# Later sums, later weight splits and earlier weight loads around the boundary of two stages of a mixture-of-experts kernel

## The chip, the core and the metric

The kernel runs on one core of one Trainium2 chip. The metric is the device time of one execution in microseconds (us); lower is better. Engines are named as in the profile: PE (matmuls, with PEld for the loads of the stationary operand), DVE (vector), ACT (scalar), POOL (GpSimd) and SP (the sync engine, which here only starts DMAs and loads registers).

## The reference

4096 tokens of width 512 pass through two blocks, each with a residual sum:

```
x = x + ffn0(moe0(x))     # moe0: (shared expert + two of eight routed experts) / 3
x = x + rnn1(moe1(x))     # moe1: one of sixteen experts by token id; rnn1: a gated recurrence
```

What matters here is the first line:

```
shared = (silu(x @ sw1.T) * (x @ sw3.T)) @ sw2.T            # 1024 hidden units
moe0   = (shared + g0 * O[e0] + g1 * O[e1]) / 3             # routed rows O, gates g0, g1
sel    = argmax(policy(moe0[:, last token of the sequence])) # one of 8 experts per sequence
h      = gelu(moe0 @ W1[sel] + b1[sel]);  r = h @ W2[sel] + b2[sel]
x      = x + moe0 + 0.3 * (r @ Wo + bo)
```

After it, `moe1` needs `sigmoid(xr @ w_recept.T)` of a mix of neighbouring tokens. A sequence is 128 tokens long; there are 32 sequences, so 32 blocks of 128 tokens.

## The kernel before

Matmuls are done in three passes on numbers split into a high and a low part (`mm3`, L66). A split (`split`, L61) is two instructions: ACT casts the source to the high part (L63), DVE subtracts it from the source (L64). Every weight and every activation goes through such a split before PE can read it.

The work stands in stages, and the change touches two of them.

**The second half of the shared expert with the sums** (L886 to L946, `shared` at L204). It runs over the four groups 4 to 7 of 512 tokens, and in each over 8 chunks of 128 hidden units, numbered 32 to 63 in all. `up` (L209) of a chunk makes two PSUM tiles `p` of 12 matmuls each; ACT and DVE turn them into the activation (`sg` at L220 to L222) and split it (`as`, L224). `down` of the chunk before (L227) adds 12 matmuls into four accumulators `acc`. The weights of these chunks are loaded once, in group 4: `fetch_sw` (L165) two chunks ahead into six raw buffers, `split_sw` (L171) one chunk ahead, into tiles `kept_u` and `kept_d` that stay for groups 5 to 7.

Beside it, `combine` (L735) does the sum for a block of 128 tokens: DVE scales the first routed row and adds the shared part (L738), adds the second routed row (L739), PE transposes the result (`pth`, L742), ACT divides by three (L744) and stores it, DVE adds the residual (L749), and SP stores that. Its inputs come from `get_o` (L718), two sums ahead, into three buffers each: two row gathers started by POOL (L722), and loads of the shared part and of x started by SP (L729, L732). The list `when` (L901 to L910) says how many sums stand behind each chunk; `hook2` (L925) does the first sum of a chunk behind it, `between` (L920) a second one within the next chunk.

In the last group `hook2` also finds the experts of the first 24 sequences (`policy`), starts the first three gathers of expert weights (`fetch_w`, L847, of 1 MB each, into three raw buffers `rawB`), and splits them (`split_w`, L866) behind chunks 4 to 6: `W1a`, `W1b` and `W2a` of the first sequence. A split frees its raw buffer, so that the gather three places later can start; the fourth and fifth gathers are for the second sequence and move nothing when its expert is the same, the sixth is `W2b`.

**The experts** (L949 to L1224). A loop over sequences b (L1156) runs `up`, `bend` (transpose, gelu, split), `down` of neighbouring sequences in turn; `used` (L1151) splits the weights three uses ahead, under a condition that skips the split when the expert does not change. In the passes b = 0 and b = 1, `weight_b` (L967) loads `Wo` and `w_recept` through the buffers `dx` and `xk` and splits them on the spot (L1170 to L1173). `Wo` is first used by `close` after b = 3, `w_recept` later still.

The order on each engine is not that of the source: a scheduler orders the instructions at build time by priorities and its own estimates of durations, and an engine then runs its list strictly in that order. `tc.issue_after(ins)` queues what is recorded within it behind `ins` on the engine of `ins`; it adds no wait.

Of the kernel before, what the change touches and what calls it, by code (L numbers as in the profile page):

```python
# [1 line left out]

# [6 lines left out]
F32 = mybir.dt.float32  # L9
# [6 lines left out]
ALU = mybir.AluOpType  # L16
# [4 lines left out]
P = 128  # L21
D = 512
KD = D // P
# [10 lines left out]
KF = F1 // P  # L34
# [14 lines left out]
def tile_kernel(ctx: ExitStack, tc: tile.TileContext, a: dict, out: bass.AP):  # L49


    nc = tc.nc
# [7 lines left out]

    def split(hi, lo, src):  # L61

        nc.scalar.copy(hi, src)  # L63
        return nc.vector.tensor_tensor(lo, src, hi.bitcast(F32), ALU.subtract).ins  # L64

    def mm3(ps, left, right, kd, start=True, stop=True):  # L66

# [78 lines left out]
    with ExitStack() as sa:  # L146
# [13 lines left out]
        NSW = KF * NG  # L160
        KEPT = KF * (NG // 2)
        sw_raw, sw_hl, x_raw, xhl = {}, {}, {}, {}
        kept_u, kept_d = {}, {}

        def fetch_sw(n, which=range(3)):  # L165
# [38 lines left out]
        def shared(groups, pools, hook, done, mid=None, before_last=None, more=False):  # L204


            tp, ps_acc, ps_mm = pools
            acts, accs = {}, {}

            def up(n):  # L210
                g, c = divmod(n, KF)
                up, dn = sw_hl.pop(n)
                ps = []
                for w in range(2):
                    ps.append(ps_mm.tile([P, GT], F32, tag="mm", name=f"p{w}_{n}"))
                    mm3(ps[w], lambda h, k: up[:, h, w, k, :], lambda h, k: xhl[g][k][:, h, :], KD)
                    if mid is not None:
                        mid(n, w)
                sg = tp.tile([P, GT], F32, tag="sg", bufs=1, name=f"sg_{n}")
                nc.scalar.activation(sg, ps[0], AF.Sigmoid)  # L220
                nc.vector.tensor_tensor(sg, sg, ps[0], ALU.mult)
                nc.vector.tensor_tensor(sg, sg, ps[1], ALU.mult)  # L222
                act = tp.tile([P, 2, GT], FR, tag="act", bufs=2, name=f"as_{n}")
                split(act[:, 0], act[:, 1], sg)  # L224
                acts[n] = (act, dn)

            def down(n):  # L227
                g, c = divmod(n, KF)
                if c == 0:
                    accs[g] = [ps_acc.tile([P, D], F32, tag="acc", name=f"acc_{g}_{j}") for j in range(GB)]  # L230
                act, dn = acts.pop(n)
                for j in range(GB):
                    mm3(
                        accs[g][j], lambda h, k: act[:, h, bass.ts(j, P)], lambda h, k: dn[:, h, :], 1,
                        c == 0, c == KF - 1,
                    )
                if c == KF - 1:
                    done(g, accs.pop(g))

            first, last = groups[0] * KF, (groups[-1] + 1) * KF - 1  # L240
            for n in range(first, last + 1):
                g, c = divmod(n, KF)
                up(n)
                if c == KF - 1 and (n < last or more):
                    split_x(g + 1)
                if n > first:
                    down(n - 1)
                if n < last:
                    split_sw(n + 1)
                if n + 1 < last:  # L250
                    fetch_sw(n + 2)
                hook(g, c)
                if c == (KF - 2 if n < KEPT + KF else 3) and (g < groups[-1] or more):
                    fetch_x(g + 1)
            if before_last is not None:
                before_last()
            down(last)
# [587 lines left out]
        AHEAD = 3  # L845
# [20 lines left out]
        def split_w(i):  # L866

            if i < len(todo):
                raw = raws.pop(i)
                kind, b = order[todo[i]]  # L870
                if b == 0:
                    ws[kind] = wh.tile([P, 2, KD, D], FR, tag="w", name=f"wB_{kind}")
                if b not in (0, PARTS[0]) and b not in changed:
                    changed[b] = nc.values_load(
                        new_i[0:1, b : b + 1], engines=[nc.scalar.engine, nc.vector.engine],
                        min_val=0, max_val=1,
                    )
                flat = ws[kind].rearrange("p h k n -> p h (k n)")
                with tc.If(changed[b] != 0) if b in changed else nullcontext():
                    for q in range(2):  # L880
                        s = bass.ts(q, KD * D // 2)
                        split(flat[:, 0, s], flat[:, 1, s], raw[:, s])
                fetch_w(i + AHEAD)


        with ExitStack() as s2:  # L886
            dn_p = s2.enter_context(tc.tile_pool(name="dn_p", bufs=2, side="right", **kw))
            split_sw(KEPT)
            pad2 = dn_p.tile([P, 320 // 4], F32, bufs=1, name="pad2")
            nc.gpsimd.memset(pad2, 0.0)  # L890
            tp = s2.enter_context(tc.tile_pool(name="tp2", bufs=2, **kw))
            cp = s2.enter_context(tc.tile_pool(name="cp", bufs=2, **kw))
            sm = s2.enter_context(tc.tile_pool(name="sm", bufs=1, **kw))
            ps_acc = s2.enter_context(tc.tile_pool(name="ps_acc2", bufs=4, space=PSUM, **kw))
            ps_mm = s2.enter_context(tc.tile_pool(name="ps_mm2", bufs=3, space=PSUM, **kw))
            ps_t = s2.enter_context(tc.tile_pool(name="ps_t2", bufs=1, space=PSUM, **kw))
            pools = (tp, ps_acc, ps_mm)


            h, last = NG // 2, NG - 1  # L900
            rest, flat, when = list(range(h * GB)), [], {}  # L901
            for g in range(h, NG):
                own = list(range((g - 1) * GB, g * GB)) if g > h else []
                for c in range(KF):
                    n = (2 if 0 < c < 3 else 0) if g == last else 1
                    n += (g == last - 1 and c == KF - 1) - (g == h and c == 0)
                    when[g, c] = []
                    for _ in range(n):
                        when[g, c].append((own if own and c > 0 else rest).pop(0))
                    flat += when[g, c]  # L910

            def sums(g, c):
                if when.get((g, c)):
                    b = when[g, c].pop(0)
                    combine(b, ps_t)
                    n = flat.index(b) + 2
                    if n < len(flat):
                        get_o(flat[n], cp, 3)

            def between(n, w):  # L920

                if w == 0:
                    sums(*divmod(n - 1, KF))

            def hook2(g, c):  # L925
                sums(g, c)
                if g == last:
                    if c == 0:
                        policy(0, PARTS[0], sm, ps_t)
                        for n in range(AHEAD):  # L930
                            fetch_w(n)
                    if 4 <= c < 4 + AHEAD:
                        split_w(c - 4)

            def keep(g, accs):
                for j in range(GB):
                    b = g * GB + j
                    shs[b] = cp.tile([P, D], F32, tag="sh", bufs=6, name=f"shc_{b}")
                    nc.scalar.copy(shs[b], accs[j])
                    if g == last:  # L940
                        i = h * GB + j
                        nc.scalar.dma_start(out=sh_d[i * P : (i + 1) * P, :], in_=shs[b])

            get_o(flat[0], cp, 3)
            get_o(flat[1], cp, 3)
            shared(range(h, NG), pools, hook2, keep, between)  # L946


    with ExitStack() as sb:  # L949
# [14 lines left out]
        PB = 2  # L964
        HF = F1 // 2

        def weight_b(name):  # L967
            pair = wb.tile([P, 2, KD, D], FR, tag=name, name=f"{name}_hl")
            flat = pair.rearrange("p h k n -> p h (k n)")
            given = a[name].rearrange("p k n -> p (k n)")  # L970
            for q, tag in enumerate(("dx", "xk")):
                s = bass.ts(q, KD * D // 2)
                raw = bp.tile([P, KD * D // 2], F32, tag=tag, name=f"raw_{name}{q}")
                nc.sync.dma_start(out=raw, in_=given[:, s])
                split(flat[:, 0, s], flat[:, 1, s], raw)
            return pair

# [178 lines left out]
        for b in range(-1, NB + 1):  # L1156
# [10 lines left out]
                used()  # L1167
            if b == -1:
                fetch_xh(0)
            if b == 0:  # L1170
                wo0 = weight_b("Wo")
            if b == 1:
                wrec = weight_b("w_recept")  # L1173

            late, step = divmod(b - 3, 3)
            if 0 <= late < GB and step == 0:
# [4 lines left out]
                policy(PARTS[0], NB, cb, ps_t)  # L1181
            if b + 1 < NB:
                bend(b + 1, "a")

            pair = b - 3 if b % 2 and 0 <= b - 3 < NB - 2 else None
            if pair is not None:
# [43 lines left out]
    with ExitStack() as sd:  # L1230
# [86 lines left out]
        AHEAD, RAW = 8, 6  # L1317
# [384 lines left out]
```

## Time and profile before

| what | us |
|---|---|
| median of three runs | 2541.81 (2541.47 to 2545.81) |
| the profiled execution, own time | 2535.17 |
| its span, first to last instruction | 2533.5 |
| PE busy in the span | 2460.9 |
| DVE busy | 1332.4 |
| ACT busy | 1064.2 |
| POOL busy | 428.5 |

The sums' stage stretches from 554.9 us of the span (first matmul of chunk 32) to 847.1 us, the experts' from there to about 1475 us. How to read the lines below: a timeline row is the start, the duration, engine, line, operation, the tile written `<-` the tiles read, and in brackets how long the engine had been idle and who ended that. A row of the windows view is the stretch, its length, the busy time of PE, PEld, DVE, ACT and POOL with the number of instructions, the clock granted to PE as a share of full speed, the share of DMA engine time, and GB/s. A row of the waits view is who waited for whom, the total, the number of times, and the longest.

### The profile page before, as it was taken

Reading aid. Unit: us, or ns where it says so; the run is one execution under the profiler, and the core shown is the slowest. Engines: PE = TensorE matmul, PEld = TensorE weight load, DVE = VectorE, ACT = ScalarE, POOL = GpSimd, SP = SyncE. Lnnn points to the kernel's source line nnn. Section 1 sums busy time; section 2 is a strip of 40 time slices with the busy share of each in tenths; the row PEclk is TensorE's granted clock in tenths of the full one; section 3 lists DMA queues with packets and bytes.
Section 4 is the critical chain, followed back from the end, with each engine's and each line's share of the span. In section 5 each row is a group of like instructions: output and inputs, shape, how many; then the busy total and the mean of one; then the engine's idle time right before and its main releaser. Section 6 shows DMA issues by size and latency. Waiting matters only on the chain. (4 is left out here: it accounts for less than half of the span.)

```text
span 2533.5 us, 37051 instructions
## 1 busy us (share of the span) xinstructions
PE 2460.9 (97%) x13044; PEld 2077.8 (82%) x13044; DVE 1332.4 (53%) x2341; ACT 1064.2 (42%) x1935; POOL 428.5 (17%) x460
## 2 busy tenths in 40 slices
PE   8999999999999899999999999999999999999996
PEld 6788899887887787888887889999978888888885
DVE  7796645556557344445444477667643333333336
ACT  5445533443224445445455466666532222222214
POOL 1000022222223223322322110000010000000003
PEclk9999999999999999999999999999999999999998
DMA  5545544557555333332243387776441111111027
GB/s 181 162 132 172 172 156 152 169 184 254 180 177 169 113 97 126 113 116 99 85 143 116 105 283 238 230 229 224 152 162 42 38 38 38 38 42 46 25 78 267
DMA packets 193116, 351.11 MB, mean 139 GB/s; under 512 B 37472, under 2 KB 72336, under 8 KB 189856
## 3 DMA queue, kind: packets, MB, share of 16 engines
q1 hardware_dynamic: 141504, 244.42, 29.0%
q0 software_dynamic: 36160, 74.90, 10.0%
q10 hardware_dynamic: 15264, 29.37, 3.3%
q8 instruction: 108, 1.77, 0.3%
q14 instruction: 80, 0.66, 0.1%
HBM read 373.94 MB, written 88.13 MB: 182 GB/s over the span
## 5 line engine op out<-in xcount | busy, mean ns | idle before, releaser
L64 DVE TENSOR_TENSOR wD<-rawD,wD 128x1024 fp32r<-128x1024 f32 x128 | 156.5, 1229 | 77.7 <-ACT wD L63 77.7
L71 PE MATMUL p<-xhl,swu 128*128 128x512 f32 x768 | 189.0, 397 | 5.3 <-ACT xhl L63 5.3
L71 PE MATMUL p<-xhl,kept_u 128*128 128x512 f32 x768 | 185.6, 397 | 0.7 <-DVE kept_u L64 0.7
L71 PEld LDWEIGHTS phD<-xe,wD 128*128 128x128 f32 x1536 | 184.7, 189 | 1.8 <-ACT xe L63 0.6
L71 PE MATMUL phD<-xe,wD 128*128 128x256 f32 x1536 | 185.7, 281 | 0.5 <-ACT xe L63 0.5
L71 PE MATMUL poD<-wD,hD 128*128 128x512 f32 x768 | 181.3, 392 | 0.0
L71 PEld LDWEIGHTS p<-xhl,swu 128*128 128x128 f32 x768 | 144.7, 191 | 36.5 <-ACT xhl L63 5.6
L71 PEld LDWEIGHTS p<-xhl,kept_u 128*128 128x128 f32 x768 | 143.3, 190 | 30.5 <-DVE kept_u L64 1.1
L71 PEld LDWEIGHTS poD<-wD,hD 128*128 128x128 f32 x768 | 141.9, 188 | 28.4
L63 ACT CAST wD<-rawD 128x1024 fp32r<-128x1024 f32 x128 | 133.2, 1047 | 53.6 <-PE poD L71 31.0
L266 POOL DMA_INDIRECT xg<-in_x_rows_dram,blk_t x71 | 67.5, 951 | 461.3 <-PE ptx L276 257.4
L1384 POOL DMA_INDIRECT y<-res_d,gat_i x32 | 32.2, 1005 | 575.0 <-DVE r L1403 496.2
L71 PE MATMUL pur<-r,xb 128*128 x852 | 117.8, 287 | 0.9 <-ACT xb L63 0.4
L71 PE MATMUL por<-r,hbr 128*128 x426 | 116.3, 407 | 1.2 <-ACT hbr L63 1.1
L64 DVE TENSOR_TENSOR xb<-ptx,xb 128x512 fp32r<-128x512 f32 x71 | 49.1, 691 | 115.3 <-ACT xb L63 113.7
L71 PEld LDWEIGHTS pur<-r,xb 128*128 128x128 f32 x852 | 104.9, 189 | 2.0 <-ACT xb L63 0.9
L71 PE MATMUL acc<-kept_d,as 128*128 128x512 f32 x384 | 96.1, 400 | 5.1 <-DVE as L64 3.1
L71 PE MATMUL poF<-z,wo_hl 128*128 128x512 f32 x384 | 96.5, 399 | 0.0
L71 PE MATMUL ps_f<-wf_hl,z 128*128 128x512 f32 x384 | 96.4, 399 | 0.0
L71 PE MATMUL ps_c<-wc_hl,z 128*128 128x512 f32 x384 | 94.9, 395 | 0.7 <-issue 0.7
L71 PE MATMUL acc<-swd,as 128*128 128x512 f32 x384 | 95.0, 392 | 0.0
L71 PE MATMUL pb<-rT,Wo_hl 128*128 128x256 f32 x768 | 94.6, 281 | 0.0
(1014 smaller groups left out, 5040.0 us busy)
## 6 DMA issues: line engine op xcount, KB each, us to landing
rawD<-in_w_key_dram SPq DMA_DIRECT2D x64, 512.0 KB
rawD<-in_w_value_dram SPq DMA_DIRECT2D x64, 512.0 KB
swr<-in_sw_dram SPq DMA_DIRECT2D x120, 256.0 KB
o_d<-obr SPq DMA_DIRECT2D x71, 256.0 KB
xraw<-in_x_dram SPq DMA_DIRECT2D x32, 256.0 KB
rraw<-in_rw_dram SPq DMA_DIRECT2D x32, 256.0 KB
xc<-in_x_dram SPq DMA_DIRECT2D x32, 256.0 KB
hid_d<-o ACTq DMA_DIRECT2D x32, 256.0 KB
```

The lines of the kernel that those rows point to most:

```text
L63: nc.scalar.copy(hi, src)
L64: return nc.vector.tensor_tensor(lo, src, hi.bitcast(F32), ALU.subtract).ins
L71: done = nc.tensor.matmul(ps, lhsT=left(hl, k), rhs=right(hr, k), start=start and k + n == 0, stop=stop and 3 * k + n == last,)
L266: nc.gpsimd.indirect_dma_start(out=xg[i], out_offset=None, in_=a["x_rows"], in_offset=bass.IndirectOffsetOnAxis(ap=blk_t[:, i : i + 1], ax ...
L1384: nc.gpsimd.indirect_dma_start(out=y, out_offset=None, in_=res_d, in_offset=bass.IndirectOffsetOnAxis(ap=gat_i[:, b : b + 1], axis=0),)
```

## The change

Three things move; no instruction is added or taken away.

- The sums. `when` puts no sum behind the first three chunks of group 4 (before: none behind the first only). The two that are left over come behind the last chunk of group 5 and behind the fourth chunk of group 6, as second sums.
- The first expert weights. `split_w` runs behind chunks 5 to 7 of the last group, not 4 to 6, and within `behind(act_split)`: on both engines its instructions are queued behind the split of the activation that was recorded last (that of the chunk itself).
- `Wo` and `w_recept`. The load is now its own function, `fetch_b`, in the passes b = 0 and b = 1, and the split (`weight_b`) comes one pass later, behind `bend` of the next sequence, again queued behind the split recorded last.

```diff
     def split(hi, lo, src):
-        nc.scalar.copy(hi, src)
-        return nc.vector.tensor_tensor(lo, src, hi.bitcast(F32), ALU.subtract).ins
+        first = nc.scalar.copy(hi, src).ins
+        done = nc.vector.tensor_tensor(lo, src, hi.bitcast(F32), ALU.subtract).ins
+        last_split[:] = first, done
+        return done
+    last_split = []
+    @contextmanager
+    def behind(both):
+        with tc.issue_after(both[0]), tc.issue_after(both[1]):
+            yield
...
                 split(act[:, 0], act[:, 1], sg)
                 acts[n] = (act, dn)
+                act_split[:] = last_split
...
                     n = (2 if 0 < c < 3 else 0) if g == last else 1
-                    n += (g == last - 1 and c == KF - 1) - (g == h and c == 0)
+                    n += (h < g < last and c == KF - 1) + (g == last - 1 and c == 3)
+                    n -= g == h and c < 3
...
-                    if 4 <= c < 4 + AHEAD:
-                        split_w(c - 4)
+                    if c >= KF - AHEAD:
+                        with behind(act_split):
+                            split_w(c - KF + AHEAD)
...
+        raw_b = {}
+        def fetch_b(name):
+            given = a[name].rearrange("p k n -> p (k n)")
+            raw_b[name] = []
+            for q, tag in enumerate(("dx", "xk")):
+                raw = bp.tile([P, KD * D // 2], F32, tag=tag, name=f"raw_{name}{q}")
+                nc.sync.dma_start(out=raw, in_=given[:, bass.ts(q, KD * D // 2)])
+                raw_b[name].append(raw)
         def weight_b(name):
             pair = wb.tile([P, 2, KD, D], FR, tag=name, name=f"{name}_hl")
             flat = pair.rearrange("p h k n -> p h (k n)")
-            given = a[name].rearrange("p k n -> p (k n)")
-            for q, tag in enumerate(("dx", "xk")):
+            for q, raw in enumerate(raw_b.pop(name)):
                 s = bass.ts(q, KD * D // 2)
-                raw = bp.tile([P, KD * D // 2], F32, tag=tag, name=f"raw_{name}{q}")
-                nc.sync.dma_start(out=raw, in_=given[:, s])
                 split(flat[:, 0, s], flat[:, 1, s], raw)
             return pair
...
-            if b == 0:
-                wo0 = weight_b("Wo")
-            if b == 1:
-                wrec = weight_b("w_recept")
...
             if b + 1 < NB:
                 bend(b + 1, "a")
+            if b in (1, 2):
+                with behind(last_split):
+                    both = weight_b(("Wo", "w_recept")[b - 1])
+                wo0, wrec = (both, None) if b == 1 else (wo0, both)
+            if b in (0, 1):
+                fetch_b(("Wo", "w_recept")[b])
```

What the scheduler makes of this differs from the source in three places that matter below. The scalings (L738) of the first two sums stand where they stood on DVE, ahead of the activation of chunk 33; only what follows them moves. In chunks 33 to 35 ACT's list now has the casts of the weights of chunks 36, 37 and 38 ahead of the casts and sigmoids of the activations. And of the two halves of the split of `W2b`, which ACT did within the last chunk before, one is now ahead of the copy `ue_0a` of the first sequence, and one behind it.

## The prediction

> **What bounds the kernel now.** I read the page first: PE is busy for 97% of the span, so a gain must come out of its 72.6 us without work, or out of work at a lowered clock. Then the waits of PE, longest first. Four rows lie in the two stages that the change touches:
>
> ```profile
> PE pt_0b L1028 <- ACT ue_0b L1021: 7.9, 1, 7.9
> ...
> PE pth L742 <- DVE o L739: 4.1, 1, 4.1
> PE acc L71 <- DVE as L64: 3.1, 2, 1.9
> ...
> PE acc L71 <- ACT as L63: 2.0, 1, 2.0
> ```
>
> The windows of 4 us around them show the second price of such a wait, the clock:
>
> ```profile
> 568.00:572.00 4.00, 1.61 (x8) 0.99 (x6) 0.40 (x1) 1.23 (x2) 0.94 (x1) 1.00 1.04 388
> 572.00:576.00 4.00, 2.33 (x9) 1.94 (x10) 4.00 (x8) 1.24 (x2) 1.04 (x1) 0.79 1.07 367
> 576.00:580.00 4.00, 4.00 (x15) 3.22 (x15) 3.14 (x9) 2.24 (x5) 0.19 (x1) 0.79 1.03 374
> ...
> 816.00:820.00 4.00, 4.00 (x11) 3.14 (x12) 3.38 (x4) 1.03 (x2) 2.88 (x2) 0.58 0.43 131
> ...
> 856.00:860.00 4.00, 0.00 (x0) 0.00 (x0) 0.12 (x1) 1.18 (x2) 0.00 (x0) 0.70 0.97 347
> 860.00:864.00 4.00, 0.93 (x5) 0.94 (x6) 3.05 (x4) 3.87 (x8) 1.01 (x1) 0.50 0.43 146
> ```
>
> The timelines of the engines tell who was late:
>
> ```profile
> 571.60 0.75 DVE L738 SCALAR_TENSOR_TENSOR o<-o,g,shc 128x512 f32<-128x512 f32 x1 [3.79 <-DMA o<-o_d,s_i]
> 599.04 0.75 DVE L739 SCALAR_TENSOR_TENSOR o<-o,g,o 128x512 f32<-128x512 f32 x1 [4.79 <-DMA o<-o_d,s_i]
> ...
> 810.50 2.00 ACT L63 CAST wB_W1b<-rawB 128x1024 fp32r<-128x1024 f32 x2 [1.91 <-DMA rawB<-in_W1b_dram,idxw]
> 813.41 0.62 ACT L63 CAST as<-sg 128x512 fp32r<-128x512 f32 x1 [0.42 <-ACT o L744]
> ...
> 858.81 1.04 ACT L63 CAST Wo_hl<-raw_Wo 128x1024 fp32r<-128x1024 f32 x1 [7.86 <-DMA sh_d<-shc]
> ```
>
> Three places, then, each an in-order engine held by a transfer while something small that PE needs stands behind. **A, 569 to 608**: DVE waits for gathered rows; DMA is full (0.87 of the engines' time in 552 to 600). PE loses 4.06 at 573.67 and 1.93 at 601.05. Lowered clock: 0.21 x 8 us = 1.68 in 572 to 580, and 0.30 x 4 + 0.12 x 4 = 1.68 in 600 to 608. Together 9.35. **B, 812 to 820**: the cast of `as` stood behind casts that waited for `W1a` and `W1b`. PE loses 2.04 + 1.16, and 0.42 x 4 = 1.68 by the clock: 4.88. **C, 855 to 868**: ACT holds the cast of `Wo`, and behind it `ue_0b`. PE loses 7.87 until 863.07, and by the clock (0.50 in 860 to 864, 0.52 in 864 to 868) some 2.4 of the 4.9 us after it: 10.3. That is 24.5 us at most.
>
> [...]in 811 to 812 POOL's weight gather moved four times what SP's queue did beside it. The DMA view of that microsecond (queue, kind: packets, MB, share):
>
> ```profile
> q0 software_dynamic: 57, 0.32, 77.2%
> q1 hardware_dynamic: 38, 0.08, 19.9%
> ```
>
> **The sums (A).** Removed from chunks 33 and 34: two transposes with their ACT and DVE work. They return behind group 5's last chunk and group 6's fourth. There PE pays the same 0.35 us for each, already in the sum, and DVE about 2.6 (0.75 + 0.75 + 1.14) in a chunk of 8.65; group 6's last chunk has two sums today and PE has no gap in 765 to 780, so I price the move at 0. POOL's first six gathers stay where they are. On SP the third sum's shared part and x go behind the weights of chunk 36: 0.5 MB less ahead of them. At some 180 GB/s for SP's queue (3.43 MB in 555 to 574) they land 2.8 us sooner, at 573.4, where ACT had them at 576.3.
>
> What remains: the two scalings still hold DVE until 572.3, so `sg` of chunk 33 is read at 572.27 to 572.95, and the second `p` tile of chunk 34, which reuses its buffer, waits from 572.2: 0.85. `as` of chunk 33 now stands on ACT behind one cast for chunk 36 (573.4 + 0.6), so 574.4 to 575.0; on DVE it ends at 576.0; PE needs the low part at about 576.3: 0.2. The sigmoid of chunk 34 stands behind all three casts of chunk 37, whose raw buffers come free at 573.5 to 575.3; 4 us of transfer each end at 579.2, the sigmoid at 580.5, its reader at 581.2, PE's need at 581.3: 0. `as` of chunk 34 likewise after chunk 38: about 0.65. Sum 1.7[...]. The second stall (599) went with a fifth gather issued at 594 into full DMA; the sums now come two chunks later, after most of the loads: 0. A gains 9.35 - 1.7 = **7.7**. Low end: transfers land no sooner than before. Then chunk 37's third piece ends its cast at 582.6, chunk 39's at 593.7, and PE waits about 2.1, 0.8 and 3; A gains 3.8.
>
> **The first weights (B).** `as` of chunk 59 now has only register loads (ten at 0.56 us each from 803.3) and the scaling of a sum ahead of it on ACT: cast by 810.5, on DVE by 811.4; PE needs it at 812.05. B gains **4.9**; low end 3, if the register loads stretch. The casts themselves (2.0 on ACT, 2.4 on DVE per weight) follow `as` of chunks 61 and 62 at 828.1 and 835.1; the next sigmoids are due at 831.1 and 839.2: covered by 1 and 2 us. `W2a` follows `as` of chunk 63: ACT 843.2 to 845.3, DVE 844.3 to 846.7, and `hidhl` of the first sequence ends at 847.4, where PE's third matmul wants it at 847.8. Covered.
>
> **The price of that (C).** The `W2b` gather can start only when `W2a`'s raw buffer is free: 846.7, not 830.8 (times of the profile of before, without the shift from A and B). Alone, that gather took from 830.8 to 836.4. Now it meets 4.2 MB (847 to 861: stores of the shared part on ACT's queue, hidden rows, x and `Wo` on SP's, two row gathers). First packet 1.7 us after the issue, 848.4; 1.05 MB of 350 GB/s is 3.0 us, and [...]4 to 5: landed at **853.3**; bounds 852.4 (as alone) and 857 (a third of the bandwidth each). Ahead of `ue_0a`, ACT casts the first half of `W2b`: 853.4 to 854.5, a branch of 0.3, `ue_0a` until 855.4. PE has six matmuls of `pu_0b` until 851.3, then waits for `pt_0a` until 855.5: a new stall of 4.2. Then ACT needs 1.05 + 1.28 (table) + 1.8 + 0.6 until `ue_0b` is done at 860.0, and PE, at half clock, is there at about 860.5, against 863.07 before.
>
> Next late: the low part of `hb_0a` stands on DVE behind the scaling of sum 28, which wants a shared part that SP loads behind `Wo`. DMA ended at 860.7; with 3 us more it lands at about 862.2, the scaling and the sum end at 863.7, `hb_0a` at 864.4. The matmuls `po` of the first sequence end at about 867 to 868 (before 869.6). C gains **2** of its 10.3; low -2 (gather at 857), high 8 (both transfers early).
>
> **`Wo` and `w_recept`.** Their casts leave 858.8 to 875, where from 867 on they hold up no one. In pass 1 ACT has hb_2a done at 884.19; 2.1 for the casts, 0.3 branch, 0.59 for `ue_2b`: 887.2, needed at 887.69. In pass 2: 899.5, needed at 900.03. Cost 0; without that half microsecond up to 1.5 each. The loads: `Wo`'s two issues (0.44 each) go ahead of hidden rows whose split comes at 873: 0. `w_recept`'s wait on SP for the buffers until `Wo` is split (886.5, 887.8); behind them stand only stores and loads that ran after 905. Landed by 892, split at 896.5: 0.
>
> **Sum.** 7.7 + 4.9 + 2 = 14.6 off the profiled execution: 2535.2 becomes 2520.6. The median lies 6.6 above that execution; I take the same amount off it: 2541.8 - 14.6 = **2527.2**.
>
> **Rivals.** (1) The boundary is free as well: `W2b` and the shared part land early, A + B + 7 = 19.6: 2522.2. For it: DVE and ACT lose 4 us of casts there. Against: full DMA from 847 to 861. (2) The first chunks stay bound by transfers, since the weights' casts now stand ahead of the activations on ACT; the change then does only in part what its words say, as its two scalings already do. A 3.8 + B 4.9 + C 0: 2533.1. For it: 0.77 MB a chunk in 8.3 us, and DMA at 1.0 today until 580. (3) Slower: `W2b` arrives so late that `ue_0a` and all behind it wait. From about 858.7 on C is a loss, 1 us for each; A and B (12.6) are eaten at 871.3 (24.6 us after the issue), and a landing at 876 gives 2546.5, 0.2% more than now. Its transfer alone took 5.7, so little speaks for it.
>
> **How the numbers follow.** Forecast 0.54, (1) 0.14, (2) 0.24, (3) 0.04, of which half lies beyond 0.2%; 0.04 for something unseen, at about no change. 0.2% is 5.1 us, about what a measurement of this kernel can tell from no change. (2) reaches to 2537, so a quarter of it counts as the same; the forecast with A at its low end is still 2531. Faster 0.54 + 0.14 + 0.17 = 0.85, same 0.12, slower 0.03. Range: from (1), with a little more of C, 2520, to the low ends of A, B and C together in (2), 2537.
>
> **What would show it.** No wait of PE for `pth` and for `as` in the sums' stage over 1.5 us, and a clock of 1.00 from 556 to the stage's end: A and B right. ACT idle before a cast of `W2b` for 2 us or more on the gather, and PE waiting for `ue_0a`: C's price right. I am wrong if `as` or `sg` waits on ACT behind `kept_u` casts for more than 2 us, if `W2b` lands within 5 us of its issue, or if `pt_2b` or `pt_3b` waits.

## The result and the profile after

The changed kernel takes 2525.71 us (median of 6 runs, 2522.89 to 2527.93) against 2541.19 for the kernel before in the same session (6 runs, 2536.3 to 2545.81): a ratio of 0.9943, 95% interval 0.9932 to 0.9953, or 15.5 us less. The profiled execution has a span of 2521.2 (before 2533.5).

The waits of PE in the changed kernel, longest first (who waited for whom, total, times, longest):

```profile
PE pt_0a L1050 <- ACT ue_0a L1043: 7.0, 1, 7.0
PE p L81 <- ACT xhl L63: 5.5, 1, 5.5
PE ptD L1304 <- DMA rowsD<-xk_d,slot_t: 3.9, 3, 1.7
```

The three rows of the first two places (`pth`, `as` on DVE, `as` on ACT) are gone; the second and third line belong to stages that the change leaves alone. The row of the third place is still on top, but with another tile: PE no longer waits for `ue_0b` behind the cast of `Wo`, it waits for `ue_0a`. The windows view of the same stretches (stretch, length, busy time of PE, PEld, DVE, ACT and POOL with the number of instructions, clock of PE, DMA share, GB/s):

```profile
568.00:572.00 4.00, 4.00 (x19) 3.34 (x18) 1.59 (x3) 0.60 (x1) 2.10 (x2) 1.00 1.06 377
572.00:576.00 4.00, 4.00 (x19) 3.16 (x19) 3.15 (x5) 1.55 (x3) 0.00 (x0) 1.00 1.03 384
576.00:580.00 4.00, 3.80 (x16) 2.52 (x15) 3.23 (x6) 3.37 (x7) 0.00 (x0) 1.00 0.89 291
816.00:820.00 4.00, 4.00 (x19) 3.30 (x18) 2.85 (x3) 1.80 (x3) 0.62 (x1) 1.00 0.00 0
...
844.00:848.00 4.00, 0.82 (x5) 0.83 (x5) 1.23 (x1) 2.51 (x3) 1.26 (x1) 0.50 1.04 419
848.00:852.00 4.00, 4.00 (x12) 3.13 (x11) 1.84 (x2) 3.72 (x9) 2.08 (x3) 0.50 0.67 218
```

From 568 to 580 PE is busy at full clock, but for 0.2 us, although the transfers are as full as before up to 576 (1.06, 1.03). Full transfers alone did not stop PE, then; the work that stood behind them did. (The new list also puts 0.5 MB of the sums' loads later. No run takes the two effects apart.) At the boundary the hole and the half clock are still there. ACT's timeline tells both halves (start, duration, operation, in brackets the idle time before and who ended it):

```profile
815.14 0.62 ACT L63 CAST as<-sg 128x512 fp32r<-128x512 f32 x1 [2.85 <-DVE sg L233]
815.66 1.99 ACT L63 CAST wB_W1a<-rawB 128x1024 fp32r<-128x1024 f32 x2
...
845.38 1.04 ACT L63 CAST wB_W2b<-rawB 128x1024 fp32r<-128x1024 f32 x1 [7.39 <-DMA rawB<-in_W2b_dram,idxw]
846.54 0.59 ACT L1043 COPY ue_0a<-pu_0a 128x512 f32<-128x512 f32 x1
```

At 815 the weights' cast follows the activation's and waits for nothing. At 845 ACT has stood 7.39 us for `W2b`, with `ue_0a` behind.

Stage times say where the 12.3 us of the two spans lie. They are taken from PE's timeline, first matmul to first matmul; "stretch" is from chunk 32 to `pu_0a` and holds the first two places, "boundary" is from `pu_0a` to `pt_1a`.

| profile | chunk 32 starts at | stretch | boundary | `pt_1a` to `pt_2b` |
|---|---|---|---|---|
| before | 554.85 | 292.45 | 22.12 | 18.27 |
| after | 557.01 | 278.97 | 21.54 | 18.26 |

The stretch can be parted between its two places by one more matmul: `pol`, the policy of the first 24 sequences, which PE does early in the last group. From chunk 32 to `pol` there are 984 matmuls in every kernel here. Up to `pol` the time fell from 223.59 to 215.65 (the first place), and from `pol` to `pu_0a` from 68.86 to 63.32 (the second).

13.5 us come from the stretch, 7.9 of them from its first place and 5.5 from its second, and 0.6 from the boundary. Chunk 32 began 2.2 us later in this execution, in stages that are the same in both kernels; that is why the spans differ by less than 14.1.

### The profile page after: what moved, and what is told of

Read it like the earlier page. It is cut to its first block, busy times and chain, and to the rows that moved or that the text cites. A ratio compares the mean times of both kernels' runs of the same rounds, so it can differ in the third digit from the quotient of the medians.

```text
span 2521.2 us, 37055 instructions
## 1 busy us (share of the span) xinstructions
PE 2455.6 (97%) x13044; PEld 2074.9 (82%) x13044; DVE 1331.5 (53%) x2341; ACT 1064.6 (42%) x1935; POOL 429.6 (17%) x460
## 3 DMA queue, kind: packets, MB, share of 16 engines
q0 software_dynamic: 36160, 74.90, 10.3%
## 5 line engine op out<-in xcount | busy, mean ns | idle before, releaser
L81 PE MATMUL pv<-w_recept_hl,xr 128*128 128x512 f32 x384 | 94.3, 395 | 0.0
```

What stands on the lines that cost most here:

```text
L81: done = nc.tensor.matmul(ps, lhsT=left(hl, k), rhs=right(hr, k), start=start and k + n == 0, stop=stop and 3 * k + n == last,)
```

## The experiments

Eleven kernels, and the changed kernel once more, in three groups; those of a group and their runs of the kernel before were on the same chip. The stages before chunk 32 ran between 554.4 and 564.1 us in these profiles with the same instructions, so I judge by the stage times and use the whole for confirmation. In brackets the stretch is parted at `pol`.

| run | stretch | boundary | to `pt_2b` | median, us | before, us | ratio (95%) |
|---|---|---|---|---|---|---|
| sums_only | 282.67 (215.69 + 66.98) | 21.63 | 18.28 | 2527.74 | 2537.81 | 0.9962 (0.9948 to 0.9975) |
| wo_only | 290.08 (221.16 + 68.92) | 19.53 | 18.34 | 2535.17 | 2537.81 | 0.9990 (0.9982 to 0.9999) |
| after_w2b_fourth | 279.23 (215.87 + 63.36) | 18.91 | 18.27 | 2521.70 | 2537.81 | 0.9931 (0.9918 to 0.9945) |
| after_splits_earlier | 279.55 (215.99 + 63.56) | 20.33 | 18.91 | 2525.02 | 2537.81 | 0.9943 (0.9929 to 0.9957) |
| fourth_sum28_later | 279.00 (215.74 + 63.26) | 12.01 | 18.26 | 2521.83 | 2541.19 | 0.9920 (0.9906 to 0.9933) |
| fourth_share_before_wo | 278.98 (215.49 + 63.49) | 13.19 | 18.27 | 2520.11 | 2541.19 | 0.9918 (0.9905 to 0.9932) |
| after_no_order | 283.07 (214.81 + 68.26) | 19.01 | 18.88 | 2531.45 | 2541.19 | 0.9969 (0.9955 to 0.9983) |
| splits_only | 285.08 (221.75 + 63.33) | 20.83 | 18.27 | 2534.74 | 2541.19 | 0.9970 (0.9960 to 0.9980) |
| after_again | 279.10 (215.79 + 63.31) | 20.33 | 18.27 | 2523.17 | 2534.74 | 0.9948 (0.9936 to 0.9960) |
| after_wo_load_late | 278.31 (214.97 + 63.34) | 20.27 | 18.27 | 2520.48 | 2534.74 | 0.9943 (0.9930 to 0.9956) |
| after_rows_late | 277.65 (214.43 + 63.22) | 21.92 | 18.26 | 2523.66 | 2534.74 | 0.9957 (0.9944 to 0.9970) |
| fourth_share_and_sum28 | 278.40 (215.10 + 63.30) | 11.99 | 18.27 | 2516.50 | 2534.74 | 0.9925 (0.9913 to 0.9937) |

**One part alone.** `sums_only` is the kernel before with the new list:

```diff
-                    n += (g == last - 1 and c == KF - 1) - (g == h and c == 0)
+                    n += (h < g < last and c == KF - 1) + (g == last - 1 and c == 3)
+                    n -= g == h and c < 3
```

> The kernel before with the new list of sums alone. Theory: the first chunks' gain comes from taking two sums out of chunks 33 and 34, with no help from the other parts. From the first matmul of chunk 32 to the first of pu_0a: 292.4 us before, 279.0 with the whole change, here 284.4 (8 of the 13.4); pu_0a to pt_1a stays at 22.1 (before 22.1, whole change 21.5). The whole: 2533, 8 us under the kernel before. Rival, that the stall in the first chunks is one of full transfers and only moves, and that most of the 13.4 belongs to the weight splits: 288 or more, the whole 2537 or more.

The stretch falls by 9.8, where the theory has 8; the boundary falls by 0.5. In the first chunks PE has one wait over 0.3 us left after chunk 32's own start (0.5, for `as`), and no window from 560 to 616 is under full clock. The wait for `as` at the first weights is still there (PE busy 1.18 of 4 us), as it must be. Up to `pol` the gain is 7.9 us, all that the whole change has there, so the theory holds. The other 1.9 us lie behind `pol`, at the wait for `as` that this edit leaves alone: it was 2.8 us here and 3.2 before, and the clock did not fall after it. That part is chance.

```profile
804.00:808.00 4.00, 1.18 (x5) 0.67 (x5) 3.35 (x7) 1.44 (x4) 0.99 (x2) 1.00 0.51 192
808.00:812.00 4.00, 4.00 (x19) 3.30 (x18) 3.14 (x5) 1.01 (x2) 2.55 (x2) 1.00 0.45 131
```

`wo_only` is the kernel before with `fetch_b` and the later split of `Wo` and `w_recept`, nothing else.

> The kernel before with the loads and splits of Wo and w_recept moved alone; the weights of the first sequence are split where they were. Theory: the boundary lost its gain to the late gather of W2b, so with W2b early the wait for pt_0b goes and no other of its size comes: pu_0a to pt_1a takes 14 us instead of 22.1 (two of the ten us stay with the low part of hb_0a, behind the scaling of sum 28); the stretch before it stays at 292.4; the whole 2533, 8 us under the kernel before. Rival, that the boundary is bound by its transfers or by the shared part of sum 28 whatever stands on ACT: pu_0a to pt_1a 20 or more, the whole 2539 or more.

The wait for `pt_0b` is gone, and a wait of 5.4 us stands in its place. PE's and DVE's timelines of this run:

```profile
860.28 4.64 PE L81 MATMUL po<-wB_W2a,hb_0a 128*128 128x512 f32 x10 [5.36 <-DVE hb_0a L64]
...
858.09 0.75 DVE L750 SCALAR_TENSOR_TENSOR o<-o,g,shc 128x512 f32<-128x512 f32 x1 [12.52 <-DMA shc<-sh_d]
```

DVE stands 12.5 us at the scaling of sum 28, whose shared part SP loads behind `xB` and `Wo`; the low part of `hb_0a` stands behind it. The boundary gains 2.6, not 8. The theory missed; the rival's cause was right, its size (20 or more) nearly. (The stretch came out 2.4 us shorter here, all of it ahead of `pol`. That is chance: the edit changes no instruction of it. The last section comes back to it.)

`splits_only` is the kernel before with the later, ordered weight splits; `Wo` is loaded and split on the spot.

> The kernel before with the later, ordered weight splits alone; list of sums as before, Wo and w_recept loaded and split on the spot. Theory: the second place alone is freed (the stretch from chunk 32 to pu_0a about 288.5, 4 under before) and at the boundary the late W2b stands where the cast of Wo stood, no more and no less: pu_0a to pt_1a 21 to 22.5. The whole 4 us under the kernel before. Rival, that the late W2b and the cast of Wo add up on ACT: 26 or more at the boundary, and the whole no faster than before.

PE waits 6.0 us for `ue_0a` behind the late `W2b`, and the boundary takes 20.8: the late `W2b` takes the place of the cast of `Wo`; the two do not add up. The stretch gained 7.4, more than the 4 expected: 5.5 behind `pol`, and 1.8 ahead of it by chance, since the first chunks happened to lose less as well (waits of 3.6 and 1.6 us, and one spell of half clock where the kernel before has two).

**Order or chunk.** Two runs take apart what freed the second place. `after_no_order` splits behind chunks 5 to 7, without the order:

```diff
-                        with behind(act_split):
-                            split_w(c - KF + AHEAD)
+                        split_w(c - KF + AHEAD)
```

> The changed kernel with the weight splits behind chunks 5 to 7, but not queued behind the activation's split. Built so, the casts of W1a and W1b stand ahead of the activation of chunk 59 on ACT, as in the kernel before. Theory: the order, not the chunk, is what freed the second place: the waits of PE for as come back there (about 3 us, with the clock 3.7 to 4.9 in the stretch from chunk 32 to pu_0a: 283 instead of 279); in turn W2b is cast in chunk 63, so the boundary is that of W2b fourth (pu_0a to pt_1a 19 instead of 21.5). The whole 1 to 2 us over the changed kernel. Rival, that by chunk 5 the weights have landed, so that the casts delay nobody: 279.5 and 19, 2.5 us under the changed kernel.

```profile
805.13 2.00 ACT L63 CAST wB_W1a<-rawB 128x1024 fp32r<-128x1024 f32 x2 [2.35 <-DMA rawB<-in_W1a_dram,idxw]
808.83 2.00 ACT L63 CAST wB_W1b<-rawB 128x1024 fp32r<-128x1024 f32 x2 [1.71 <-DMA rawB<-in_W1b_dram,idxw]
```

ACT again waits for both gathers ahead of the activation, PE waits 1.5 and 1.2 us for `as`, and the stretch is 4.1 longer: the scheduler pulls the casts forward unless they are queued behind something. The loss lies behind `pol` (68.3 for 63.3). Stage by stage it is as expected (283 and 19). The whole came out 5 to 7 us over the changed kernel by the ratios, of which these stages explain 2 to 3; the rest isn't accounted for, and is about as large as the intervals of the ratios.

`after_splits_earlier` keeps the order and goes back to chunks 4 to 6 (`if 4 <= c < 4 + AHEAD`, `split_w(c - 4)`):

> The changed kernel with the three weight splits behind chunks 4 to 6 again, as in the kernel before, yet queued behind the activation's split. Theory: what made the second place free is the order behind the activation, not the chunk; one chunk (8.3 us) sooner W2b lands by 838, before ACT needs to cast it: stretch from chunk 32 to pu_0a 279.0 as with the change, pu_0a to pt_1a 14 instead of 21.5, the whole 2518. Rivals: the weights have not landed by then and ACT holds the next sigmoid for them (stretch of 281 or more); or the boundary stays as it is for other transfers (20 or more): 2524 or more.

The stretch stays at 279.5: the order is what matters, the chunk is not. `W2b` is now early and `pt_0b` comes 7.8 us after `pu_0a` instead of 17.6, but the boundary takes 20.3, not 14: `po` waits 6.1 us for `hb_0a`, and the second rival had its size.

**What is behind the late `W2b`.** `after_w2b_fourth` gathers it two chunks sooner:

```diff
-        todo = [0, 1, 3, 2, *range(4, len(order))]
+        todo = [0, 1, 3, 5, 2, 4, *range(6, len(order))]
```

> The changed kernel, but W2b of the first sequence is gathered fourth, not sixth: it takes the raw buffer that W1a leaves, two chunks (about 16 us) sooner. Theory: the wait for ue_0a (7.0 us) and the half clock after it go, pu_0a to pt_1a takes 14 us instead of 21.5, the stretch before stays at 279.0: the whole 2518, 7.5 under the changed kernel (23 under the kernel before). Rival, that the transfers at the boundary or the shared part of sum 28 hold the first sequence back anyway: 20 or more, the whole 2524 or more.

`pt_0a` and `pt_0b` come 4.2 and 7.8 us after `pu_0a`, with no wait. Of the 7.5 us expected only 2.6 arrive. DVE's timeline, then PE's:

```profile
847.92 0.75 DVE L750 SCALAR_TENSOR_TENSOR o<-o,g,shc 128x512 f32<-128x512 f32 x1 [6.16 <-DMA shc<-sh_d]
...
850.11 4.59 PE L81 MATMUL po<-wB_W2a,hb_0a 128*128 128x512 f32 x10 [4.60 <-DVE hb_0a L64]
```

It is the same wait as in `wo_only`: with the first obstacle gone, sum 28 is the next. My theory had put it at 2 us, although the prediction had named it as "next late". Two runs test that. `fourth_sum28_later` also queues that sum behind the split of `hb_0a` (`first_hb` is set in `bend` for the first half of sequence 0):

```diff
-                combine(NB - GB + late, ps_t)
+                with behind(first_hb) if late == 0 else nullcontext():
+                    combine(NB - GB + late, ps_t)
```

> The changed kernel with W2b gathered fourth, and the sum of block 28 queued on DVE, ACT and PE behind the split of hb_0a. Theory: in the run with W2b fourth, DVE stood 6.2 us at the scaling of sum 28, waiting for its shared part, and hb_0a's low part stood behind it; with the order turned round the wait of po (4.6 us) and the half clock after it go, and nothing else of that size is late: pu_0a to pt_1a 12.5 us instead of 18.9, the whole 6 under the run with W2b fourth, about 2515. Rival, that the scaling, now ahead of hb_0b, only moves the wait to the second down matmuls (hb_0b): pt_1a at 12.5, but pt_1a to pt_2b 21 or more instead of 18.3, and no more than 3 us in all.

The boundary takes 12.0 and PE waits for nothing in it; `pt_1a` to `pt_2b` stays at 18.26. The cause is shown. The whole did not show it (2521.83; the ratio fell by 0.0011, some 3 us for the 6 expected, and the intervals overlap), with chunk 32 starting at 564.1 in its profile. `fourth_share_before_wo` leaves DVE's order alone and turns SP's round:

```diff
+            if b == -1:
+                get_o(NB - GB, cb, 1)
...
-                fetch_b(("Wo", "w_recept")[b])
+                with tc.issue_after(share[0]) if b == 0 else nullcontext():
+                    fetch_b(("Wo", "w_recept")[b])
```

> The changed kernel with W2b gathered fourth, and the rows, shared part and x of sum 28 loaded ahead of Wo on SP's queue. Theory: what makes the shared part late is that 1 MB of Wo stands ahead of it; it now lands about 3 us sooner (845 instead of 847.9), the wait of po shrinks from 4.6 to about 1.5 us and with it the half clock: pu_0a to pt_1a 14 us instead of 18.9, the whole 4 to 5 under the run with W2b fourth. Rival, that all the loads at the boundary share the transfer engines and the shared part lands when it did: 18 or more, no gain.

The boundary takes 13.2, with 0.9 us of waiting left:

```profile
850.76 2.58 PE L81 MATMUL po<-wB_W2a,hb_0a 128*128 128x512 f32 x10 [0.90 <-DVE hb_0a L64]
```

A load of 1 MB ahead of the shared part on SP's queue was the reason for its lateness. What is left comes from the row gathers of sum 28, for which DVE stands 1.7 and 0.8 us there. Both edits and the changed kernel once more, on one chip:

> The changed kernel once more, on the chip of the three runs beside it. The same stage times as in its first profile: 279.0 us from chunk 32 to pu_0a, 21.5 from pu_0a to pt_1a; W2b landed 9.7 us after its issue; 15 us under the kernel before, as before.

> The changed kernel with W2b gathered fourth, the loads of sum 28 ahead of Wo, and the sum of block 28 behind the split of hb_0a. Theory: with any one of the two edits to sum 28 the boundary is nearly empty (12.0 and 13.2 us), so together they give 12.0 and the whole 1 us under the run with the loads alone: some 20 under the kernel before and 6 to 8 under the changed kernel. Rival, that the order behind hb_0a makes a wait later in the stage (the run with it alone came out 1.7 us above the run with the loads alone): 12.0 at the boundary, but the whole no faster than with the loads alone.

`after_again` repeats the stretch; at the boundary it has 20.3, since less of it ran at half clock (6.8 us for 10.2, by the windows view). The version with both edits has the lowest median here: 2516.5 against 2523.17, 6.7 us under the changed kernel on the same chip. That it beats the loads alone is not shown: the ratios are 0.9925 and 0.9918, on different chips, though from chunk 32 to `pt_3b` it takes 321.0 us for 322.8. The later wait of the rival does not show either: behind `pt_3b` it takes 1633.4 us, and the other profiles 1632.4 to 1636.1. DVE takes the split first and finds the shared part landed when it comes to sum 28 (0.21 before it is a branch):

```profile
846.13 0.69 DVE L64 TENSOR_TENSOR hb_0a<-hf_0a,hb_0a 128x512 fp32r<-128x512 f32 x1 [1.99 <-ACT hb_0a L63]
...
847.64 0.75 DVE L750 SCALAR_TENSOR_TENSOR o<-o,g,shc 128x512 f32<-128x512 f32 x1 [0.21 <-DVEq L891]
```

**Why the gather took so long.** In the changed kernel `W2b` lands 9.7 us after its issue. Two runs take one neighbour away each: `after_wo_load_late` the 1 MB of `Wo` (its loads go behind `hidB` of sequence 3 on SP), `after_rows_late` the two row gathers of sum 28 (queued on POOL behind the gather of `W2a` of sequence 1; the sum itself behind `hb_0a`).

> The changed kernel, with the loads of Wo queued on SP behind the hidden rows of sequence 3, about 17 us later, so that 1 MB less is under way beside the gather of W2b and ahead of the shared part of sum 28. Built so, the scaling of sum 28 stands on DVE ahead of the low part of W2b. Theory: W2b landed late (9.7 us after its issue) because it shares the engines with what the boundary loads beside it; without Wo it lands about 7.5 us after the issue, the wait for ue_0a shrinks from 7.0 to about 5, pu_0a to pt_1a 19 instead of 21.5, the whole 2 under the changed kernel. Rival, that W2b shares its own queue with the row gathers and Wo takes nothing from it: 9.5 us and 21.5, no gain.

> The changed kernel, with the two row gathers of sum 28 issued on POOL some passes later, and that sum behind the split of hb_0a. Theory, that what slows W2b is the 0.5 MB of rows in its own queue: W2b lands about 7 us after its issue instead of 9.7, and pu_0a to pt_1a falls to 19. Rival, that the transfers on SP's and ACT's queues slow it: 9 us or more, and 21 or more. If both take part, each of these two runs shows some of it.

The issue on POOL and the cast that waits for it on ACT, first of `after_wo_load_late`:

```profile
832.37 1.20 POOL L863 DMA_INDIRECT rawB<-in_W2b_dram,idxw  x1 [7.17 <-DVE wB_W2a L64]
...
841.70 1.04 ACT L63 CAST wB_W2b<-rawB 128x1024 fp32r<-128x1024 f32 x1 [7.03 <-DMA rawB<-in_W2b_dram,idxw]
```

and of `after_rows_late`:

```profile
834.14 1.20 POOL L863 DMA_INDIRECT rawB<-in_W2b_dram,idxw  x1 [7.17 <-DVE wB_W2a L64]
...
843.90 1.04 ACT L63 CAST wB_W2b<-rawB 128x1024 fp32r<-128x1024 f32 x1 [7.46 <-DMA rawB<-in_W2b_dram,idxw]
```

9.3 and 9.8 us from issue to cast, against 9.7 (845.38 - 835.70) in the changed kernel and 9.6 in `after_again`. Neither neighbour alone is the reason; both theories fall. (`splits_only`, with both neighbours, had 8.7, so the time varies by as much as these differences.) The gap from 21.5 to 20.3 at the boundary of `after_wo_load_late` is that of `after_again` too, so it is no gain either. What else is under way are the stores of the shared part, hidden rows and x; taking all of it away at once was not tried.

## Why the prediction was right, step by step

**A, the first chunks (forecast 7.7 of 9.35).** Right in mechanism, and in size for this pair of profiles: up to `pol` the changed kernel is 7.9 under before, and so is `sums_only`. But 3.36 of the 9.35 was the clock, and that part is luck. The other two kernels with the old list take 221.2 and 221.8 up to `pol`, where before took 223.6, and the eleven profiles with the new one 214.4 to 216.0; so the list is worth 5 to 9, by the execution. What I left for PE to wait was 1.7. The waits found are 0.5 in the changed kernel, for `as` (0.2 and 0.3), and the 12 matmuls behind each take 3.29 us for 2.88, so it was about 1.3. That such waits bring no half clock was an assumption; here every window from 556 to 616 is at 1.00. The 0.85 us for the second `p` tile of chunk 34 did not come in this profile; in three others with the new list PE has a wait of 0.3 to 0.8 us before a `p` tile of these chunks. (The waits at the low end, 2.1, 0.8 and 3, would leave 3.45, not 3.8.) The rival that the first chunks stay bound by transfers is refuted: DMA share 1.06, and PE with hardly a gap. One sign of being wrong came by its letter: the sigmoid of chunk 34 could run from about 574.4, when its 12 matmuls end, and ran at 581.07, behind casts of weights. It cost PE nothing. The forecast itself had this sigmoid late and covered, so the sign was badly chosen.

**B, the first weights (forecast 4.9).** Mechanism right, size a little low: from `pol` to `pu_0a` it is 68.9 before and 63.3 in the changed kernel, 5.5 us, and 63.3 in `splits_only`. `after_no_order`, which takes the order away, has 68.3. `sums_only` has 67.0, since the clock did not fall there: the half clock, 1.68 of the 4.9, does not come each time.

**C, the boundary (forecast 2 of 10.3).** Right that it is a loss of some 10: emptied, the boundary takes 11.99 where it took 22.12. Right that the change gets little of it, and why: it gained 0.6 in the first profile and 1.8 in the second. The first is the fair one beside the forecast of 2, since PE ran 10.2 us at half clock in it, as before, and 6.8 in the second. Inside this step one term was too small and another did not bind. I had `W2b` land 6.6 us after its issue (846.7 to 853.3): first packet after 1.7, transfer 4 to 5 (an estimate: 3.0 at 350 GB/s, and some for the other queues). It was 9.7:

```profile
835.70 1.20 POOL L863 DMA_INDIRECT rawB<-in_W2b_dram,idxw  x1 [7.17 <-DVE wB_W2a L64]
```

By the trace its first packet starts at 839.02, 3.3 us after the issue, its last ends at 844.8, and the cast begins 0.5 us later. The queues of 841 to 843, with `W2b` under way in POOL's queue q0 (DMA view: packets, MB, share):

```profile
q0 software_dynamic: 56, 0.46, 67.8%
q1 hardware_dynamic: 57, 0.12, 17.6%
q10 hardware_dynamic: 56, 0.11, 14.7%
```

The three queues moved 56 or 57 packets each in these 2 us, POOL's of 8 KB and the others of 2 KB, and POOL's has 68% of the share. My bound of a third of the bandwidth for each was wrong in its reason. It came out near the landing, 857 against 856.4, because the start was 1.6 us later than I had it and the transfer took 5.8. The row gathers behind `W2b` in its queue did not hold it up: their packets begin at 843.3, with 0.94 MB of its 1.05 moved. So PE waited 7.0 for `ue_0a`, not 4.2. The second term, `hb_0a` behind sum 28, I put at 864.4; in the changed kernel it did not bind, since everything ahead of it was 3 us later, and `po` starts without a wait. That the two errors nearly cancel is luck. With `W2b` early it binds at once, 4.6 to 6.1 us in four runs.

**`Wo` and `w_recept` (forecast 0).** Right: `pt_1a` to `pt_2b` 18.26 after, 18.27 before, and 12.34 us on to `pt_3b` in both. The half microsecond of slack in each pass was enough.

**The sum.** 14.6 forecast; from chunk 32 to `pt_2b` 332.84 became 318.77, 14.1 us, and 317.7 in the second profile; the medians differ by 15.5. By parts it was 7.9, 5.5 and 0.6 for the 7.7, 4.9 and 2 of the forecast: the errors of B and C have different signs and cancel in part. The profiled execution came to 2522.89, with 2520.6 forecast; 2.2 of that difference lie ahead of chunk 32. The rival that has the boundary free needed the two further edits. The slower rival had the right wait, and `W2b` did land within 2.3 us of the 858.7 from which C would have been a loss. The prediction prices such a landing in two ways that don't fit together: at 857 it has C at -2, and by this limit still at a gain. With 856.4 C was +0.6, so the -2 was too low.

## What to carry to other kernels

When an engine runs its list in order, a cast that waits for a transfer must stand behind the small work that the bottleneck engine needs next; say so in the program (a queue order), since moving the source line alone left the order as it was. A buffer freed later starts the next gather later (here that of `W2b`, 16.5 us ahead of `pu_0a` in the kernel before, 0.3 us ahead of it in the changed one): before delaying a consumer, look for the load that reuses its buffer, and which burst it will then meet. When one stall of a stage boundary is removed, follow the next late input at once; here the first two of three obstacles could be taken away for some 3 us together, and the third gave the other 7.

## What the runs showed of the hardware

- The clock's price for a wait was not fixed by its length. In the kernel before 1.93 us of waiting were followed by 1.68 us of loss at half clock. In `wo_only` PE was held 3.0 and 3.6 us in the same chunks and the clock stayed at 1.00 in every window from 556 to 616. The 1.93 us of before, then the 3.6 us of `wo_only`:

```profile
596.00:600.00 4.00, 3.12 (x14) 2.25 (x12) 0.96 (x2) 0.00 (x0) 0.63 (x2) 1.00 0.99 259
600.00:604.00 4.00, 2.95 (x8) 2.36 (x9) 4.00 (x10) 0.60 (x1) 0.00 (x1) 0.70 0.60 204
...
596.00:600.00 4.00, 0.84 (x4) 0.37 (x2) 1.57 (x3) 0.22 (x1) 0.19 (x1) 1.00 0.84 287
600.00:604.00 4.00, 3.56 (x18) 2.95 (x19) 3.91 (x9) 0.60 (x1) 0.61 (x1) 1.00 0.57 186
```

- In these profiles the price goes with where the wait falls. In the packed traces of before and of the changed kernel the granted clock changes 21 and 15 times, and within each trace all the changes lie on a grid of 3.413 us, to 0.001 us. In the kernel before it goes to half at 574.28, 601.59, 816.63 and 857.59: the distances, 27.31, 215.04 and 40.96, are 8, 63 and 12 times 3.413. In the rows of the table with a fall, it comes at the end of a step of the grid in which PE stood for 1.93 us or more. The steps of before are read from its trace; those of `splits_only` and `wo_only` are an estimate, counted from the one fall that their windows show (at 580.6, and at 813.8 with 0.72 in 812 to 816):

| run | PE stood (us) | steps of the grid | idle in them | half clock after |
|---|---|---|---|---|
| before | 569.6 to 573.7 | 570.9 to 574.3 | 2.80 | yes |
| before | 599.1 to 601.1 | 598.2 to 601.6 | 1.93 | yes |
| before | 812.0 to 814.1, 814.8 to 816.0 | 813.2 to 816.6 | 2.03 | yes |
| splits_only | 577.4 to 581.1 | 577.2 to 580.6 | 3.2 | yes |
| wo_only | 569.9 to 573.0 | 568.0 to 571.4, 571.4 to 574.8 | 1.5, 1.5 | no, no |
| wo_only | 596.8 to 600.4 | 595.3 to 598.7, 598.7 to 602.1 | 1.9, 1.7 | no, no |

  In the traces of before and of the changed kernel, from 30 us on to the last matmul, the clock fell after each of the 14 steps at full clock with 1.93 us idle or more, after one of the three with 1.56 to 1.63 (1.58), and after none with 1.25 or less. (The ends of matmuls are modelled in the trace, so the figures are no sharper than that.) This describes the two traces; that it holds elsewhere is not shown. The waits of 3.0 and 3.6 us that the grid cuts in two cost nothing by the clock, the 1.93 us within one step cost 1.7. The two executions of the changed kernel did not meet the grid in the same place (the clock falls 6.4 and 7.3 us after `pu_0a`), so a forecast should hold the clock's part as a range: by these runs, from nothing to 1.7 for waits of 2 to 4 us. Half clock lasted 3.4 us after the three waits of before in the stretch. At the boundary it lasted 10.2 us in the kernel before (wait of 7.9 us) and in the changed kernel (7.0), and 6.8 in `after_again` (6.8) and in `after_w2b_fourth` (4.6).
- The first packet of the `W2b` gather came 0.7 us after POOL's issue ended in the kernel before (831.75 to 832.44), ahead of the boundary, and 2.1 us after it in the changed kernel (836.90 to 839.02), at the full boundary. The transfer took 4.0 us in the first (to 836.44) and 5.8 in the second (to 844.83). In `after_rows_late`, without the row gathers behind it, POOL's queue moved 1.04 MB in 837.4 to 843.5, with the issue ended at 835.34. The cause of the late start wasn't tried; in the changed kernel ACT's queue, with the stores of the shared part, and SP's moved 1 MB (0.71 and 0.26) between the start of the issue and that first packet.
- The stages ahead of the change start the sums' stage anywhere from 554.4 to 564.1 us with the same instructions (561.0 to 564.1 in the four profiles of the second group, 554.4 to 559.4 in the others), and what lies behind `pt_3b` takes 1632.4 to 1636.1. A difference of a few microseconds is read from stage times, not from one span.
